# A hybrid layer stack with a selective scan on one core: ScalarE's share of stage work set by the kind of units, all front stages first, two turn stages beside others, a DRAM buffer for every image

## The chip, the cores and the metric

The kernel runs on one core of one Trainium2 chip. The core has a matrix engine (PE in the profile), VectorE (DVE), ScalarE (ACT), GpSimd (POOL), and SyncE (SP), which in this kernel issues every DMA. The metric is the device time of one execution in microseconds; the number that counts is the median of several runs.

## The reference

Four images of 96 channels and 64 x 64 pixels pass through four layers. Cut to what is computed:

```python
# layer 0: group norm, 1x1 conv to 192 channels, depthwise 3x3, silu, then a selective scan
u  = silu(depthwise3x3(Win @ gn(x)) + conv_b)            # (b, 192, 64, 64)
xs = [u by rows, u by columns, both of them reversed]    # K = 4 sequences of L = 4096
dt, B, C = split(sel_w[k] @ xs[k])                       # 6, 16 and 16 rows
delta = softplus(dt_w[k] @ dt + dt_b)
h[t]  = h[t-1] * exp(delta[t] * A) + (delta[t] * xs[t]) * B[t]   # 192 channels x 16 states
y[t]  = sum over the states of h[t] * C[t]  (+ Ds * xs)
x = x + Wout @ layernorm(y0 + y1 + y2 + y3, turned back to rows)
# layer 1: inverted residual: 1x1 conv to 576, depthwise 3x3, 1x1 conv back, residual
# layer 2: spectral block: w1, relu, FFT over 4096 tokens, complex diagonal, relu, inverse FFT, w2;
#          then a feed-forward with values rounded to 8-bit floats
# layer 3: attention without softmax (6 heads), then a second such feed-forward
```

The scan of layer 0 has 4 images x 4 sequences x 192 channels x 16 states, each 4096 steps long. It is most of the work.

## The kernel before

**Units of the scan.** `scans` cuts the scan into steps of 512 positions: 4 images x 4 sequences x 8 chunks = 128 steps. Every step has 12 units of two 128 x 512 tiles (a tile is 32 channels x 4 states), so there are 1536 units; the text calls the turn of the main loop that starts unit n "slot n". One unit costs: a product `db` on GpSimd (L1266); two `exp` on ScalarE (L1276, function `decays`) into PSUM tiles `ps_da`; two scans on VectorE (L1285, function `states`); a product with C, which gives `hc`; and eight small matmuls that sum over the states for a pair of units (L1330). Two kinds of unit alternate. In a "pool" unit (numbers 1, 3, 5, 7 and 10 of 12, `POOL_C`) GpSimd makes the product with C (L1306) and copies the last state (L1302). In the other seven, VectorE makes the product (two L1290) and ScalarE copies the last state (two L1300, function `keep`). `ps_da` has four banks, which is two units.

**ScalarE's order.** Inside a slot the kernel emits, in this order: `decays` for the next unit, ahead of which stand the copies `keep` of the previous one if that was not a pool unit; the copy `yt` of finished sums (L1344, function `sums_out`); the inputs of later units; the scans of this unit; sums; and at last the stage work. Every engine runs its instructions in the order written.

**Stages.** All other work is cut into streams of small pieces, grouped into stages: `front` (input convolution, silu, and the scan's inputs delta, delta times u, B and C, which are stored to DRAM as `d_delta`, `d_du` and `d_bc`), `turn` (adds the column sequences' outputs, turned back to rows, to the others), `conv` (layer norm of layer 0's output and layer 1), two `spectral` stages, `layer_2`, `product` and `layer_3`. A stage begins when the stage before it has ended; inside a stage up to `width` streams run side by side. `middle(b)` is turn and conv of image b, `layers_2_and_3(b)` the rest; `plan` lists the stages. The turn of images 2 and 3 already runs beside layer 3 of the image before, as stage `layer_3_turn`; the turn of images 0 and 1 is a stage of its own with one stream.

**The planner.** Each piece names an engine and a rough cost in microseconds. At the end of each slot `advance` takes pieces from the first stage's streams for as long as the budget `owed` lasts (`RATE`, 6.0 per slot, more near the end) and the piece fits its engine's `room`. Room grows in each slot by the first number of `SHARE` and is capped by the second: for ScalarE 2.4 and 2.8. A piece fits if room is at least half of its cost. So `SHARE` says how much stage work stands between the `decays` of two slots. When the scan has ended, what is left of the last image (`behind`, and layers 2 and 3 of image 3) is emitted with nothing beside it.

**Buffers.** `big` gives two large SBUF tiles (6144 floats per partition); a front holds both, as `ua` and `ub`, and uses 4096 columns of each. `turn` takes one as `ya`. `tmp` is a ring of 10 tiles of 512 columns. `d_delta`, `d_du` and `d_bc` have three images' worth in DRAM, so image 3 takes image 0's place.

Of the kernel before, what the change touches and what calls it, by code (L numbers as in the profile page):

```python
# [27 lines left out]
B, C, H, W = 4, 96, 64, 64  # L28
L = H * W
# [22 lines left out]


WORK = {"weights": 47.0, "turn": 79.2, "front": 417.0, "conv": 447.0,
        "spectral": 111.2, "layer_2": 231.0, "product": 1.2, "layer_3": 153.6, "layer_3_turn": 232.8}
RATE = 6.0
SHARE = {"pe": (3.0, 3.2), "act": (2.4, 2.8), "dve": (1.5, 2.0)}
NQ, NG, NPAIR = 4, HID // 32, H // 2


# [35 lines left out]
def hybrid_kernel(ctx: ExitStack, tc: tile.TileContext, a: dict):  # L96
# [111 lines left out]
    def images(name, shape, zero=None, sets=2):  # L208

        out = []  # L210
        for i in range(sets):
            t = dram1.tile(shape, F32, name=f"{name}{i}")
            if zero is not None:
                zero(t)
            out.append(t)
        return out

    d_delta = [images(f"delta{k}_", [NCH, DI, CH], sets=3) for k in range(K)]
    d_du = [images(f"du{k}_", [NCH, DI, CH], sets=3) for k in range(K)]
    d_bc = [images(f"bc{k}_", [NCH, 2 * NS, CH], sets=3) for k in range(K)]  # L220

# [353 lines left out]

    def scan_inputs(b, u, o, c, done):

        i = b % 3  # L580
        if not done.issuperset([c] if o == 0 else range(NCH)):
            while not done.issuperset([c] if o == 0 else range(NCH)):
                yield wait(1)
            yield wait(2)
        ua, ub = u
        yield pe(1.8, 1)
        p = bank()
        mm(p, lhsT=sel[:, o, 0, :], rhs=view(ua, o, c), start=True, stop=False)
        mm(p, lhsT=sel[:, o, 1, :], rhs=view(ub, o, c), start=False, stop=True)

        yield ac(0.7)
        xd = tmp("xd")
        act(xd, p, AF.Identity, bias=col("one"))
        free()
        for e in (0, 1):
            later(d_bc[o + 2 * e][i][c], xd[64 * e : 64 * e + 2 * NS])
        for part in range(3):
            yield pe(0.9, 1, part > 0)
            p = bank()
            if part < 2:  # L600
                mm(p, lhsT=dtw[:, o + 2 * part, 0:128], rhs=xd, start=True, stop=True)  # L601
                at = [(slice(0, 128), o + 2 * part, slice(0, 128))]
            else:
                for e in (0, 1):
                    mm(p[64 * e : 64 * e + 64], lhsT=dtw[:, o + 2 * e, 128:DI], rhs=xd, start=True, stop=True)
                at = [(slice(64 * e, 64 * e + 64), o + 2 * e, slice(128, DI)) for e in (0, 1)]

            yield ac(0.65)
            z = tmp("z")
            act(z, p, AF.Abs)  # L610
            yield ac(0.65)
            act(z, z, AF.Exp, scale=-1.0)
            yield ac(0.65)
            act(z, z, AF.Ln, bias=1.0)  # L614
            yield dv(0.7)
            nc.vector.scalar_tensor_tensor(p, p, 0.0, z, ALU.max, ALU.add)  # L616
            yield dv(0.85)
            g = tmp("g")
            nc.vector.tensor_mul(split(g), split(p), view(ub if part == 2 else ua, o, c))
            for rows, k, ch in at:  # L620
                later(d_du[k][i][c][ch], g[rows])
            yield ac(0.6)
            nc.scalar.copy(z, p)  # L623
            free(behind=True)
            for rows, k, ch in at:
                later(d_delta[k][i][c][ch], z[rows])
        traced[b].add((o, c))

    def turn(b):


        im = b % 2
        early = b == B - 1
        while scanned[b] < (2 if early else 3) * NCH:
            yield wait(1)
        t = big("ya")
        for r in (2, 0, 1) if early else (0, 1, 2):
            lo = 64 * r
            for at, k in ((0, 1), (64, 3)):
                load(t[at : at + 64, :L].rearrange("p (c l) -> p c l", c=NCH),  # L640
                     d_y[k][im][:, lo : lo + 64, :].rearrange("c p l -> p c l"))

            rows = not (early and r == 2)
            held = slice(0 if rows else 64, 128)

            def fetch(c):
                u = t[:, L + c % 4 * CH : L + c % 4 * CH + CH]
                if rows:
                    load(u[:64], d_y[0][im][c, lo : lo + 64])
                load(u[64:], d_skip[b][c, lo : lo + 64])  # L650
                return u

            def added(p, of):
                c, u = of
                mm(split(p[:64]), lhsT=const("two")[:, :64],  # L655
                   rhs=t[:, :L].rearrange("p (w h) -> p h w", h=H)[:, c * RPC : (c + 1) * RPC, :], start=True, stop=False)
                mm(p[:64], lhsT=skips[held, r], rhs=u[held], start=False, stop=True)

            def stored(p, of):
                s = tmp("yrow")[:64]  # L660
                nc.scalar.copy(s, p[:64])
                later(d_yt[im][of[0]][lo : lo + 64], s)

            chunks = ahead(1, fetch, range(NCH))

            ready = (lambda n: scanned[b] >= 2 * NCH + min(n + 2, NCH)) if early and rows else (lambda n: True)
            yield wait(10)
            yield from in_turn(chunks, pe(2.7, 1), added, ac(0.6), stored, ready=ready)
            yield wait(2)

# [398 lines left out]
    def layers_2_and_3(b):  # L1069
# [83 lines left out]
        else:  # L1153
# [1 line left out]
        return spectra + [  # L1155
            Stage("layer_2", 4 if b == B - 1 else 3, *(layer_2(c) for c in range(NCH))),
            Stage("product", 1, product()),
            Stage("layer_3", 4 if b == B - 1 else 3, *(layer_3(c) for c in range(NCH))) if b not in (1, 2) else
            Stage("layer_3_turn", 4, turn(b + 1), *(layer_3(c) for c in range(NCH))),
        ]  # L1160

    def front(b):


        u, there, done = [], set(), set()

        def memory():
            u.extend([big("ua")[:, :L], big("ub")[:, :L]])
            if b > 0:
                yield from normalised(b, arriving(b), there)  # L1170
                return

            chunks = [(c, fetch_image(b, c, tmp)) for c in range(NCH)]
            load(cst[:, CS["grp"]], a["cst"][:, CS["grp"]])
            load(cols, a["cols"])
            first_weights()
            yield from group_norm(b, chunks)
            yield from normalised(b, chunks, there)

        streams = [memory()]  # L1180
        for c in range(0, NCH, 2):
            streams.append(input_conv(b, u, c, there, done))
            for e in (c, c + 1):
                streams.append(scan_inputs(b, u, 0, e, done))
        streams += [scan_inputs(b, u, 1, c, done) for c in range(NCH)]
        return [Stage("front", 3 if b == 0 else 4, *streams)]


# [5 lines left out]

    def middle(b):

        return ([] if b >= 2 else [Stage("turn", 1, turn(b))]) + conv_block(b)

    def plan():

        stats = (group_norm(b, arriving(b)) for b in range(1, B))
        out = [Stage("weights", 2, later_weights(), *stats)] + front(1) + front(2)
        out += middle(0) + layers_2_and_3(0) + front(3)
        for b in (1, 2):
            out += middle(b) + layers_2_and_3(b)
        return out

    def scans(stages):
# [22 lines left out]

        def load_states(step, j):
            t = pair("rep_BC")
            of = d_bc[step["k"]][step["b"] % 3][step["c"], 8 * j : 8 * j + 8].rearrange("(s e) l -> s (e l)", e=2)
            load(t.rearrange("p e l -> p (e l)"), of.unsqueeze(0).to_broadcast([32, 4, 2 * CH]))
            step["BC"][j] = t

        def load_channels(step, i, name):
            t = pair(f"rep_{name}")
            of = (d_delta if name == "d" else d_du)[step["k"]][step["b"] % 3][step["c"], 64 * i : 64 * i + 64]  # L1240
            load(t.rearrange("p e l -> p (e l)"),
                 of.rearrange("(p e) l -> p (e l)", e=2).unsqueeze(1).to_broadcast([32, 4, 2 * CH]))
            step[name][i] = t
# [95 lines left out]
        def sums_out():  # L1339
            while summed:  # L1340
                group, y = summed.pop(0)
                step = group[0]["step"]
                yt = sp.tile([128, CH], F32, name="yt")
                nc.scalar.copy(yt, y)  # L1344
                to = d_y[step["k"]][step["b"] % 2][step["c"]]
                for m in (0, 1):
                    at = 128 * group[0]["pass"] + 64 * m
# [13 lines left out]
        for slot in range(len(units) + 6):  # L1361
# [26 lines left out]
                states(x)  # L1388
            for group in due.get(slot, ()):
                sums(group)  # L1390
            for e, (us, most) in SHARE.items():
                room[e] = min(room[e] + us, most)
            tensor[0] = 0.0
            held_banks[0] -= freed[0]
# [8 lines left out]


    clock, tensor = [-1], [0.0]
    room = {e: most for e, (_, most) in SHARE.items()}

    class Stage:

# [233 lines left out]
```

## Time and profile before

| what | value |
|---|---|
| median of 3 runs | 6344.4 us (6340.63 to 6344.61) |
| the profiled execution | 6358.61 us, its span 6356.8 us |
| first scan to last scan's unit | 81.2 to 5912.6 us of the span |
| after the scan | 444.2 us |
| VectorE busy | 5490.6 us (86% of the span) |
| GpSimd busy | 5169.6 us (81%) |
| ScalarE busy | 4191.3 us (66%) |

All times below are of the span. VectorE's instructions L1285 come two per unit, so their order in the trace tells when each slot began; with the order of the program, this gives each stage's slots and times:

| stage | slots | from, to (us) | us per slot |
|---|---|---|---|
| front of images 1 and 2 | 112 to 305 | 617.3 to 1418.4 | 4.15 |
| turn of image 0 | 305 to 355 | 1418.4 to 1593.4 | 3.50 |
| conv of image 0 | 355 to 489 | 1593.4 to 2046.1 | 3.38 |
| spectral of image 0, two stages | 489 to 557 | 2046.1 to 2307.4 | 3.84 |
| layer_2 of image 0 | 557 to 619 | 2307.4 to 2531.3 | 3.61 |
| layer_3 of image 0 | 626 to 669 | 2554.1 to 2709.8 | 3.62 |
| front of image 3 | 669 to 769 | 2709.8 to 3116.6 | 4.07 |
| turn of image 1 | 769 to 819 | 3116.6 to 3300.6 | 3.68 |
| layer_3_turn (images 1 and 2) | 1089 to 1147 | 4274.9 to 4504.7 | 3.96 |
| conv of image 3, up to the last unit | 1477 to 1536 | 5709.6 to 5912.6 | 3.44 |

In the profile's groups, "out<-in xcount | busy, mean ns" is followed by the idle time of the engine just ahead of these instructions and by what ended it. In windows, each row is a stretch with the busy time and number of instructions of every engine, the granted clock of the matrix engine, the share of the DMA engines and GB/s.

### The profile page before, as it was taken

Reading aid. Unit: us, or ns where it says so; the run is one execution under the profiler, and the core shown is the slowest. Engines: PE = TensorE matmul, PEld = TensorE weight load, DVE = VectorE, ACT = ScalarE, POOL = GpSimd, SP = SyncE. Lnnn points to the kernel's source line nnn. Section 1 sums busy time; section 2 is a strip of 40 time slices with the busy share of each in tenths; the row PEclk is TensorE's granted clock in tenths of the full one; section 3 lists DMA queues with packets and bytes.
Section 4 is the critical chain, followed back from the end, with each engine's and each line's share of the span. In section 5 each row is a group of like instructions: output and inputs, shape, how many; then the busy total and the mean of one; then the engine's idle time right before and its main releaser. Section 6 shows DMA issues by size and latency. Waiting matters only on the chain. (4 is left out here: it accounts for less than half of the span.)

```text
span 6356.8 us, 84759 instructions
## 1 busy us (share of the span) xinstructions
PE 4685.7 (74%) x27692; PEld 1723.3 (27%) x27692; DVE 5490.6 (86%) x6059; ACT 4191.3 (66%) x8072; POOL 5169.6 (81%) x2743
## 2 busy tenths in 40 slices
PE   6732767756888776686469878767898777679998
PEld 2100212201222642121012236321222552112274
DVE  4979898998999989989989998888999999889245
ACT  5743777765666677877546656767666667666435
POOL 4857878779999899987899998898999988889100
PEclk9855978867998888797779987878899887789999
DMA  5654565667754554456776445456754554566201
GB/s 178 206 167 146 190 204 187 201 201 221 221 162 151 183 181 156 151 193 208 212 213 197 156 152 192 157 162 199 225 171 159 171 192 141 172 209 202 84 13 39
DMA packets 430397, 1100.47 MB, mean 173 GB/s; under 512 B 74138, under 2 KB 75904, under 8 KB 428804
## 3 DMA queue, kind: packets, MB, share of 16 engines
q1 hardware_dynamic: 429956, 1095.06, 54.3%
q8 instruction: 220, 3.60, 0.2%
q14 instruction: 221, 1.81, 0.1%
HBM read 861.88 MB, written 237.44 MB: 173 GB/s over the span
## 5 line engine op out<-in xcount | busy, mean ns | idle before, releaser
L1266 POOL TENSOR_TENSOR db<-rep_g,rep_BC 128x1024 f32<-128x1024 f32 x1536 | 3607.0, 2365 | 689.1 <-DVE hc L1285 323.5
L1276 ACT ACTIVATE ps_da<-rep_d,aneg 128x512 f32<-128x512 f32 x3072 | 2061.8, 690 | 478.8 <-DVE hc L1285 347.2
L1285 DVE TENSOR_TENSOR_SCAN ps_da<-ps_da,state,db 128x512 f32<-128x512 f32 x1568 | 1923.9, 1272 | 274.3 <-ACT state L1300 151.4
L1306 POOL TENSOR_TENSOR hc<-hc,rep_BC 128x1024 f32<-128x1024 f32 x640 | 1511.2, 2361 | 49.3 <-DVE hc L1285 4.5
L1285 DVE TENSOR_TENSOR_SCAN hc<-ps_da,state,db 128x512 f32<-128x512 f32 x1120 | 1371.7, 1266 | 71.3 <-issue 20.6
L1330 PE MATMUL ps_y<-hc,cst 128*32 128x512 f32 x6144 | 1014.4, 739 | 566.2 <-POOL hc L1306 261.1
L1290 DVE TENSOR_TENSOR hc<-ps_da,rep_BC 128x512 f32<-128x512 f32 x1792 | 1135.5, 675 | 0.0
L1300 ACT COPY state<-ps_da 128x1 f32<-128x1 f32 x1568 | 246.3, 157 | 456.9 <-DVE hc L1290 455.4
L1330 PEld LDWEIGHTS ps_y<-hc,cst 128*32 128x32 f32 x6144 | 145.8, 118 | 1210.5 <-issue 438.2
L810 PE MATMUL ps_mm<-h,wd 128*32 128x512 f32 x3120 | 357.0, 593 | 7.0 <-ACT r L155 7.0
L550 PE MATMUL ps_mm<-xp,taps 128*128 128x512 f32 x576 | 294.7, 656 | 54.9 <-ACT ua L552 15.1
L1285 DVE TENSOR_TENSOR_SCAN ps_da<-ps_da,db 128x512 f32<-128x512 f32 x224 | 261.3, 1212 | 39.5 <-ACT state L1300 24.7
L787 PE MATMUL ps_mm<-wd,w 128*32 128x512 f32 x1984 | 254.9, 630 | 29.3 <-DMA wd<-x 20.0
L601 PE MATMUL ps_mm<-xd,dtw 128*128 128x512 f32 x256 | 168.5, 751 | 73.6 <-ACT z L623 53.5
L791 ACT ACTIVATE h<-ps_mm 128x512 f32<-128x512 f32 x261 | 151.8, 597 | 66.5 <-PE ps_mm L787 64.5
L869 PE MATMUL ps_mm<-r,cst 128*128 128x512 f32 x222 | 152.3, 778 | 56.5 <-ACT acc L892 14.2
L616 DVE SCALAR_TENSOR_TENSOR ps_mm<-ps_mm,z 128x512 f32<-128x512 f32 x192 | 131.7, 686 | 70.8 <-ACT z L614 67.0
L1285 DVE TENSOR_TENSOR_SCAN hc<-ps_da,db 128x512 f32<-128x512 f32 x160 | 186.2, 1204 | 6.1 <-issue 3.1
L655 PE MATMUL ps_mm<-ya,cst 128*64 128x512 f32 x192 | 183.1, 1044 | 10.4 <-ACT acc L892 10.4
L610 ACT ACTIVATE z<-ps_mm 128x512 f32<-128x512 f32 x192 | 114.1, 595 | 111.7 <-PE ps_mm L601 59.2
L982 PE MATMUL ps_mm<-wa,xp 128*64 128x96 f32 x1728 | 134.9, 318 | 64.6 <-DVE d L987 61.9
L550 PEld LDWEIGHTS ps_mm<-xp,taps 128*128 128x128 f32 x576 | 115.9, 208 | 229.5 <-issue 159.9
(348 smaller groups left out, 6675.9 us busy)
## 6 DMA issues: line engine op xcount, KB each, us to landing
rep_BC<-bc SPq DMA_DIRECT2D x512, 512.0 KB
rep_g<-du SPq DMA_DIRECT2D x384, 512.0 KB
rep_d<-delta SPq DMA_DIRECT2D x384, 512.0 KB
y<-yt SPq DMA_DIRECT2D x512, 128.0 KB
du<-g SPq DMA_DIRECT2D x128, 256.0 KB
delta<-z SPq DMA_DIRECT2D x128, 256.0 KB
tab<-in_etab SPq DMA_DIRECT2D x112, 256.0 KB
ya<-y SPq DMA_DIRECT2D x24, 1024.0 KB
```

The costliest lines, as they stand in the source:

```text
L550: mm(p, lhsT=taps[:, t, 0:128], rhs=window(t, c + e), start=t == 0, stop=t == 8)
L601: mm(p, lhsT=dtw[:, o + 2 * part, 0:128], rhs=xd, start=True, stop=True)
L655: mm(split(p[:64]), lhsT=const("two")[:, :64], rhs=t[:, :L].rearrange("p (w h) -> p h w", h=H)[:, c * RPC : (c + 1) * RPC, :], start=True, ...
L787: mm(p[32 * n : 32 * n + 32], lhsT=w1[:, 32 * g : 32 * g + 32], rhs=xin[:, n : n + 15 : 2, 1 : W + 1], start=True, stop=True)
L810: mm(p[32 * n : 32 * n + 32], lhsT=held["wd"][:, groups[i], o, dx, :], rhs=here[i][:, :, dx : dx + W], start=dx == 0, stop=dx == 2)
L1266: nc.gpsimd.tensor_mul(x["db"], x["step"]["g"][x["i"]], both(x["step"]["BC"][x["j"]][:, 0]))
L1276: act(x["da"][e], x["step"]["d"][x["i"]][:, e], AF.Exp, scale=aneg[:, av : av + 1])
L1285: nc.vector.tensor_tensor_scan(x["h"][e][:, order], x["da"][e][:, order], x["db"][:, e, order], start, ALU.mult, ALU.add)
L1290: x["made"] = nc.vector.tensor_mul(x["hc"][:, e], x["h"][e], x["step"]["BC"][x["j"]][:, 1])
L1300: nc.scalar.copy(to[:, e : e + 1], x["h"][e][:, end : end + 1])
L1306: x["made"] = nc.gpsimd.tensor_mul(x["hc"], x["hc"], both(x["step"]["BC"][x["j"]][:, 1]))
L1330: done = mm(y[32 * q : 32 * q + 32], lhsT=const("stack"), rhs=x["hc"][:, e], start=first or (x["pass"] == 0 and x["j"] == 0), stop=last or ...
```

## The change

Five edits:

- **ScalarE's share** depends on two things: whether this slot's unit is a pool unit, and whether the next one is. Pool then not pool: 2.8 per slot, capped at 3.0. Not pool then pool: 1.2, capped at 1.6. Two alike: 2.4 and 2.8, as before.
- The copy of finished sums on ScalarE takes 0.6 from ScalarE's room.
- **All fronts first**: the front of image 3 follows that of image 2, ahead of the conv of image 0.
- **Two turns moved**: the turn of image 0 runs as a second stream of image 3's front, in the unused columns of `ua` and `ub` (two halves of 2048 columns each, so its loads and its strided matmuls come in two halves; its small input `u` comes from the `tmp` ring). The turn of image 1 runs beside layer 3 of image 0, as the others did.
- `d_delta`, `d_du` and `d_bc` have an image's worth of DRAM for each of the four images.

```diff
-SHARE = {"pe": (3.0, 3.2), "act": (2.4, 2.8), "dve": (1.5, 2.0)}
+SHARE = {"pe": (3.0, 3.2), "dve": (1.5, 2.0)}
+SHARE_ACT = {(True, False): (2.8, 3.0), (True, True): (2.4, 2.8), (False, False): (2.4, 2.8), (False, True): (1.2, 1.6)}
...
-    d_delta = [images(f"delta{k}_", [NCH, DI, CH], sets=3) for k in range(K)]
+    d_delta = [images(f"delta{k}_", [NCH, DI, CH], sets=B) for k in range(K)]
...
-        i = b % 3
+        i = b
...
-    def turn(b):
+    def turn(b, rooms=()):
...
-        t = big("ya")
+        if rooms:
+            of_rows = [t[:, L:] for t in rooms]
+        else:
+            t = big("ya")
+            of_rows = [t[:, :L]]
+        each = L // len(of_rows)
...
-            for at, k in ((0, 1), (64, 3)):
-                load(t[at : at + 64, :L].rearrange("p (c l) -> p c l", c=NCH),
-                     d_y[k][im][:, lo : lo + 64, :].rearrange("c p l -> p c l"))
+            for n, part_of in enumerate(of_rows):
+                cs = slice(n * each // CH, (n + 1) * each // CH)
+                for at, k in ((0, 1), (64, 3)):
+                    load(part_of[at : at + 64].rearrange("p (c l) -> p c l", l=CH),
+                         d_y[k][im][cs, lo : lo + 64, :].rearrange("c p l -> p c l"))
...
-                u = t[:, L + c % 4 * CH : L + c % 4 * CH + CH]
+                u = tmp("yu") if rooms else t[:, L + c % 4 * CH : L + c % 4 * CH + CH]
...
-                mm(split(p[:64]), lhsT=const("two")[:, :64],
-                   rhs=t[:, :L].rearrange("p (w h) -> p h w", h=H)[:, c * RPC : (c + 1) * RPC, :], start=True, stop=False)
-                mm(p[:64], lhsT=skips[held, r], rhs=u[held], start=False, stop=True)
+                wide_of = W // len(of_rows)
+                mm(p[:64], lhsT=skips[held, r], rhs=u[held], start=True, stop=False)
+                for n, part_of in enumerate(of_rows):
+                    mm(split(p[:64])[:, :, n * wide_of : (n + 1) * wide_of], lhsT=const("two")[:, :64],
+                       rhs=part_of.rearrange("p (w h) -> p h w", h=H)[:, c * RPC : (c + 1) * RPC, :], start=False,
+                       stop=n == len(of_rows) - 1)
...
-            Stage("layer_3", 4 if b == B - 1 else 3, *(layer_3(c) for c in range(NCH))) if b not in (1, 2) else
+            Stage("layer_3", 4 if b == B - 1 else 3, *(layer_3(c) for c in range(NCH))) if b == B - 1 else
             Stage("layer_3_turn", 4, turn(b + 1), *(layer_3(c) for c in range(NCH))),
...
+        if b == B - 1:
+            return [Stage("front_turn", 5, streams[0], turn(0, rooms), *streams[1:])]
         return [Stage("front", 3 if b == 0 else 4, *streams)]
...
-        return ([] if b >= 2 else [Stage("turn", 1, turn(b))]) + conv_block(b)
+        return conv_block(b)
...
-        out = [Stage("weights", 2, later_weights(), *stats)] + front(1) + front(2)
-        out += middle(0) + layers_2_and_3(0) + front(3)
+        out = [Stage("weights", 2, later_weights(), *stats)] + front(1) + front(2) + front(3)
+        out += middle(0) + layers_2_and_3(0)
...
                 nc.scalar.copy(yt, y)
+                room["act"] -= 0.6
...
-            for e, (us, most) in SHARE.items():
+            of = (x is not None and x["pool"], slot + 1 < len(units) and units[slot + 1]["pool"])
+            for e, (us, most) in (SHARE | {"act": SHARE_ACT[of]}).items():
                 room[e] = min(room[e] + us, most)
```

More of the change, by code (lines that the diff above doesn't have):

```diff
@@ L54 @@
 WORK = {"weights": 47.0, "turn": 79.2, "front": 417.0, "conv": 447.0,
-        "spectral": 111.2, "layer_2": 231.0, "product": 1.2, "layer_3": 153.6, "layer_3_turn": 232.8}
+        "spectral": 111.2, "layer_2": 231.0, "product": 1.2, "layer_3": 153.6, "layer_3_turn": 232.8, "front_turn": 496.2}
 RATE = 6.0
-SHARE = {"pe": (3.0, 3.2), "act": (2.4, 2.8), "dve": (1.5, 2.0)}
+SHARE = {"pe": (3.0, 3.2), "dve": (1.5, 2.0)}
+SHARE_ACT = {(True, False): (2.8, 3.0), (True, True): (2.4, 2.8), (False, False): (2.4, 2.8), (False, True): (1.2, 1.6)}
 NQ, NG, NPAIR = 4, HID // 32, H // 2
@@ L216, in images @@
         return out
-    d_delta = [images(f"delta{k}_", [NCH, DI, CH], sets=3) for k in range(K)]
-    d_du = [images(f"du{k}_", [NCH, DI, CH], sets=3) for k in range(K)]
-    d_bc = [images(f"bc{k}_", [NCH, 2 * NS, CH], sets=3) for k in range(K)]
+    d_delta = [images(f"delta{k}_", [NCH, DI, CH], sets=B) for k in range(K)]
+    d_du = [images(f"du{k}_", [NCH, DI, CH], sets=B) for k in range(K)]
+    d_bc = [images(f"bc{k}_", [NCH, 2 * NS, CH], sets=B) for k in range(K)]
     d_y = [images(f"y{k}_", [NCH, 256, CH]) for k in range(K)]
@@ L1162, in front @@
     def front(b):
-        u, there, done = [], set(), set()
+        u, rooms, there, done = [], [], set(), set()
         def memory():
-            u.extend([big("ua")[:, :L], big("ub")[:, :L]])
+            rooms.extend([big("ua"), big("ub")])
+            u.extend([t[:, :L] for t in rooms])
             if b > 0:
@@ L1233, in load_states @@
             t = pair("rep_BC")
-            of = d_bc[step["k"]][step["b"] % 3][step["c"], 8 * j : 8 * j + 8].rearrange("(s e) l -> s (e l)", e=2)
+            of = d_bc[step["k"]][step["b"]][step["c"], 8 * j : 8 * j + 8].rearrange("(s e) l -> s (e l)", e=2)
             load(t.rearrange("p e l -> p (e l)"), of.unsqueeze(0).to_broadcast([32, 4, 2 * CH]))
@@ L1239, in load_channels @@
             t = pair(f"rep_{name}")
-            of = (d_delta if name == "d" else d_du)[step["k"]][step["b"] % 3][step["c"], 64 * i : 64 * i + 64]
+            of = (d_delta if name == "d" else d_du)[step["k"]][step["b"]][step["c"], 64 * i : 64 * i + 64]
             load(t.rearrange("p e l -> p (e l)"),
@@ L1405, in hybrid_kernel @@
     clock, tensor = [-1], [0.0]
-    room = {e: most for e, (_, most) in SHARE.items()}
+    room = {e: most for e, (_, most) in SHARE.items()} | {"act": 2.8}
     class Stage:
```

## The prediction

> **What bounds the kernel now.** I read the busy shares first, then windows cut where the scan begins and ends, then VectorE's waits, then windows by stage.
>
> ```profile
> PE 4685.7 (74%) x27692; PEld 1723.3 (27%) x27692; DVE 5490.6 (86%) x6059; ACT 4191.3 (66%) x8072; POOL 5169.6 (81%) x2743
> ```
>
> Two engines are near the top, VectorE and GpSimd. Cutting the span at the first scan and after the last unit:
>
> ```profile
> 81.20:5912.60 5831.40, 4222.50 (x23410) 1470.96 (x23412) 5311.74 (x5729) 3981.36 (x7745) 5157.52 (x2735) 0.82 0.58 183
> 5912.60:6356.80 444.20, 412.64 (x4154) 231.67 (x4146) 164.20 (x301) 181.64 (x286) 0.00 (x0) 0.98 0.14 43
> ```
>
> The third busy time is VectorE's: 5311.7 of 5831.4 us while the scan runs, so 519.7 us idle. In the second row it is hardly used; there the matrix engine works 412.6 of 444.2 us. So the time of the scan part is VectorE's busy time plus its idle time, and PE sets the rest. VectorE's own waits say what the idle time is:
>
> ```profile
> DVE ps_da L1285 <- ACT state L1300: 176.1, 111, 10.5
> DVE ps_da L1285 <- ACT ps_da L1276: 56.8, 40, 4.4
> DVE st L501 <- DMA x<-in_x: 40.5, 1, 40.5
> DVE ps_da L1285 <- POOL db L1266: 38.8, 34, 7.6
> DVE ps_mm L616 <- ACT z L614: 30.3, 20, 4.0
> ```
>
> Over 230 us are scans that wait for ScalarE, though ScalarE is the less busy engine: it is late, not full. Three stages, in windows:
>
> ```profile
> 1418.40:1593.40 175.00, 102.86 (x296) 18.17 (x296) 154.11 (x160) 89.00 (x191) 167.90 (x93) 0.72 0.71 212
> 1593.40:2046.10 452.70, 392.91 (x2280) 114.35 (x2280) 430.76 (x466) 302.25 (x595) 449.03 (x237) 0.91 0.58 181
> ...
> 4274.90:4504.70 229.80, 172.06 (x455) 39.74 (x454) 192.98 (x202) 165.24 (x330) 195.51 (x105) 0.82 0.67 198
> ```
>
> First a turn alone: GpSimd is busy 168 of 175 us, VectorE 154. Then a conv, where GpSimd is full (449 of 453). Then layer 3 with a turn, where neither is (VectorE 193 of 230). In the turn ScalarE has little to do (89 us), and still scans wait for it. The reason is in ScalarE's waits there:
>
> ```profile
> ACT yrow L661 <- PE ps_mm L657: 42.9, 20, 14.0
> ACT state L1300 <- DVE hc L1290: 28.4, 14, 3.8
> ```
>
> ScalarE stands at the turn's eviction while PE waits for the turn's loads, and the next unit's `exp` stands behind it.
>
> **What the Trainium skill says.** "PSUM — Partial Sum Buffer", section "Engine vs sequencer instructions", has ScalarE's and VectorE's queues strictly first in, first out, and matmuls starting and ending in program order. The trace agrees: see L661 above. So stage work ahead of an `exp` delays a scan although ScalarE is 66% busy. "Perfetto Trace Analysis", section "Optimization Strategy", says that regimes with different contended engines can be improved by interleaving them. Here it bears on the turns: a slot asks 3.36 us of GpSimd (167.9/50 in the turn; 5157.5/1536 over all) and, without stage work, 3.08 of VectorE (154.1/50). In a turn or a conv GpSimd binds, in a front VectorE (379.9 of 416.9 us in 1001.5 to 1418.4). The 100 slots of the two turns so leave VectorE 100 x 0.28 = 28 us idle, which go if they run beside fronts and layer 3. That is part of the turns' idle time below and isn't added to it.
>
> **The change, part by part.** No scan work is added or taken away, so I sum three things: what moves behind the last scan, what VectorE's idle time becomes, and small additions.
>
> *1. What moves behind the scan.* ScalarE's income was 2.4 per slot. It becomes (5 x 2.8 + 5 x 1.2 + 2 x 2.4)/12 = 2.07, less two copies of 0.6 per 12 slots: 1.97. Stages that used it up get longer: in the two programs' order, fronts of images 1 and 2 take 105 and 107 slots instead of 91 each (112 to 203, 204 to 295), the six spectral stages 231 instead of 204 (waits between them included), layer_2 70 instead of 62. The two turns alone, 100 slots, go; image 3's front with a turn takes 119, each layer_3_turn 61 instead of 58. Summed, the conv of image 3 begins at slot 1499, before at 1477. It then moves at the same pace (3.3 planned us per slot in both), so more of it is left after the last unit. Counting matmuls after the last one of L1330: 2351 instead of 2178, 173 more. They are 84 of L810 (four run side by side), 64 of L787 (the same) and 25 of full width. Prices from the timeline of PE in this very stretch: 12 of L810 take 2.58 us (6015.24 to 6017.81), 4 of L787 take 0.87 us (6053.99 to 6054.87), one full one 0.86 us (6084.36 to 6085.22). Sum: 7 x 2.58 + 16 x 0.87 + 25 x 0.86 = 18.1 + 13.9 + 21.5 = 53.5 us. Nothing hides it: PE is busy 171.2 of 175.4 us in the stretch 5912.6 to 6088.0. +54 us. With it eight VectorE instructions of about 0.65 us leave the scan part: -5 us.
>
> *2. VectorE's idle time.* Stage work emitted in slot s stands ahead of the `exp` that the scan of slot s+2 needs. I took the idle time of VectorE ahead of each scan from the trace, and sorted it by kind of slot s, by stage, and by the planned ScalarE work of slot s. In all, 381 us (weights and product left out). Slots "not pool, then pool" carry 269 of it: 49 in fronts, 61 in spectral, 26 in layer_2, 33 in conv, 100 in turns and layer 3. There the `exp` of slot s+2 has only a pool unit's two scans (2 x 1.27 us) to hide in, and two state copies (0.16 each) precede it. In spectral the step is plain: 0 us per slot with up to 1.2 us planned, 0.68 with 1.8 to 2.4, 3.96 with 2.4 to 3.0. The new order puts at most 1.8 or so into such slots. Multiplying the new counts by the old means: fronts 29, spectral 1, layer_2 19, conv 31, layer 3 with turn 49, plus 10 that I take for the turn in the front: 139, so 130 less.
>
> The other slots carried 112 us (fronts 35, spectral 25, layer_2 13, conv 19, rest 20). Pool slots followed by another kind now get up to 3.0: some 87 slots at 3 us or more, of which the trace has few. Their price is open: 0.0 us in six spectral slots, 1.58 in six of front. So 0 to 137 us; I take 0.5 each, 44 us, since a long unit (two scans and two L1290, 3.9 us) then covers the `exp`. With the old means for the rest I get 138 us, 26 more.
>
> Together 104 us less. A cruder sorting without stages gives 64 for the shares alone. I take 85, with 15 to 150 as ends: turns that stall behind their loads do so beside layer 3 too (36.8 and 42.3 us of idle time in the two layer_3_turn stages, 8.2 in the layer_3 alone, about 18 and 20 in the turns), so there the sorting is the least sure.
>
> *3. Additions with one answer.* Image 0's turn in halves: 24 more matmuls (L655 takes 1035 ns for 512 strided columns, so halves cost about the same together; PE has slack there) and six more loads (626 ns of SP each, spread over 119 slots): 0; uncovered, 6 x 0.63 = 4 us. Fourth DRAM images: other addresses, no instruction; without them image 3's front, at slot 338, would overwrite what the scan of image 0 still reads, up to slot 384. The turn's input in the `tmp` ring: its load waits on SP for a tile of ten uses back, with `rep` loads queued behind it, and GpSimd waits for those (the trace has 116.8 us of such waits on `rep_BC`, hidden mostly). Bound: 0 to 24 x 1 us; I take 0.
>
> Sum on the profiled execution: 6356.8 + 54 - 5 - 85 = 6321 us of span, -36. The profiled run (6358.6) stands 14 us above the median 6344.4; applying -36 there gives **6308 us**.
>
> **Rivals.**
> *A, slower: the later conv decides.* The place is the stretch after the last scan, the price 54 us of PE work with nothing beside it. It decides as soon as idle time falls by less than 49 us. For it: stalls that come from PE and DMA stay, and the cap of 3.0 opens new ones; at 1.58 us per such slot part 2 gives only about 10 us. Against: the spectral numbers above. With 25 us regained: 6344 + 54 - 5 - 25 = 6368.
> *B, nothing: gain and cost cancel.* VectorE's work is the same, and a stall removed on ScalarE often becomes one on GpSimd (scans wait on `db` 57 us in all), and the four convs stay with GpSimd. 6344 +- 13.
> *C, much faster.* If alternating shares clear nearly all of the 230 us on ScalarE, idle time falls by 150 or more: 6344 + 49 - 150 = 6243. Against: turns' waits on loads, 40.5 us of the weights stage (loads of rows on SP), which nothing touches.
> That the turns aren't really interleaved is excluded by the order of instructions.
>
> **How the numbers follow.** Forecast 0.48, A 0.26, B 0.14, C 0.12. Range: my ends for idle time, 15 to 150, give 6378 and 6243; cutting the rare tail of C, 6255 to 6378. A measurement of this kernel tells 0.2% (13 us) from no change; faster is the forecast and C, 0.60, same 0.14, slower 0.26.
>
> **What would show it.** Scans' waits on `state` L1300 and on `ps_da` should fall from 233 us to about 150; spectral windows from 3.84 us per slot to about 3.6; the stretch after the last unit should grow from 444 to about 498 us, nearly all PE; layer_3_turn should come three times with 25 to 40 us idle each. The prediction is wrong if the stretch after the scan grows by much less than 54 us, if scans still wait on ScalarE for 200 us, or if GpSimd's waits on `rep` grow in the front with a turn.

## The result, and the profile after

The changed kernel takes 6329.83 us (median of 13 runs, 6317.88 to 6334.25). The kernel before, run beside it 13 times, takes 6335.24 us (6323.9 to 6344.61). The ratio is 0.999, with a 95% interval of 0.9981 to 0.9998: some 5 us, where 36 us were forecast. The profiled execution of the changed kernel took 6329.87 us (span 6328.1), which is its median. That of the kernel before, 6358.6 us, was 23 us above its own median.

The changed kernel in windows, cut at the first scan and at the end of the last one (columns as before: stretch, its length, then busy time of PE, PE's weight loads, VectorE, ScalarE and GpSimd, the granted clock, DMA share, GB/s):

```profile
79.30:5828.10 5748.80, 4136.25 (x23110) 1441.46 (x23106) 5300.57 (x5720) 3958.34 (x7709) 5159.94 (x2735) 0.83 0.58 186
5828.10:6328.10 500.00, 469.38 (x4505) 250.84 (x4504) 170.20 (x311) 203.80 (x321) 0.00 (x0) 0.99 0.13 41
```

Beside the two rows of before: the scan part went from 5831.4 to 5748.8 us, and VectorE's idle time in it (length less busy time) from 519.7 to 448.2 us. The stretch behind the last scan went from 444.2 to 500.0 us, and PE is busy in all but 31 us of it. So both things happened that the prediction summed. VectorE's waits while the scan runs show where the idle time changed:

```profile
DVE ps_da L1299 <- ACT ps_da L1290: 70.1, 39, 9.7
DVE ps_da L1299 <- ACT state L1314: 68.0, 45, 8.2
DVE hc L1299 <- issue: 60.3, 44, 13.2
DVE hc L1299 <- ACT ps_da L1290: 54.2, 18, 6.9
DVE st L502 <- DMA x<-in_x: 41.0, 1, 41.0
```

L1299 is the scan (L1285 before), L1314 the state copy, L1290 the `exp`. The wait on state copies fell from 176.1 to 68.0 us. But scans that write `hc`, which are those of the pool units, now wait 54.2 us for the `exp`, and 60.3 us for something that the view doesn't name ("issue"). The same two waits in the kernel before:

```profile
DVE hc L1285 <- issue: 23.7, 32, 3.0
DVE hc L1285 <- ACT ps_da L1276: 9.2, 4, 3.0
```

The timeline settles the unnamed one: each of these 44 scans of the changed kernel starts 0.09 us after an `exp` has ended, so they waited for ScalarE too. The late work moved from the one kind of unit to the other.

By stage, VectorE's idle time, the first trace of before against the changed kernel: fronts of images 1 and 2, 65 to 39 us; spectral 87 to 64; layer_2 56 to 27. Against that, the front of image 3 and the turn of image 0, 51 us as two stages, became 69 as one; and layer_3, the turn of image 1 and two layer_3_turn, 119 us, became three layer_3_turn with 126.

### The profile page after: what moved, and what is told of

It is laid out like the page before. It is cut to its first block, busy times and chain, and to the rows that moved or that the text cites. A ratio compares the mean times of both kernels' runs of the same rounds, so it can differ in the third digit from the quotient of the medians.

```text
span 6328.1 us, 84866 instructions
## 1 busy us (share of the span) xinstructions
PE 4655.2 (74%) x27740; PEld 1712.8 (27%) x27740; DVE 5485.5 (87%) x6059; ACT 4190.5 (66%) x8072; POOL 5171.6 (82%) x2743
## 5 line engine op out<-in xcount | busy, mean ns | idle before, releaser
L1290 ACT ACTIVATE ps_da<-rep_d,aneg 128x512 f32<-128x512 f32 x3072 | 2063.6, 689 | 507.8 <-DVE hc L1299 361.0
L1299 DVE TENSOR_TENSOR_SCAN ps_da<-ps_da,state,db 128x512 f32<-128x512 f32 x1568 | 1921.2, 1270 | 143.5 <-ACT ps_da L1290 54.0
L1299 DVE TENSOR_TENSOR_SCAN hc<-ps_da,state,db 128x512 f32<-128x512 f32 x1120 | 1371.0, 1265 | 135.6 <-issue 57.2
L1314 ACT COPY state<-ps_da 128x1 f32<-128x1 f32 x1568 | 245.5, 157 | 410.5 <-DVE hc L1304 408.4
L821 PE MATMUL ps_mm<-h,wd 128*32 128x512 f32 x2976 | 342.0, 592 | 7.0 <-ACT r L156 7.0
L551 PE MATMUL ps_mm<-xp,taps 128*128 128x512 f32 x576 | 287.9, 641 | 44.6 <-ACT xp L531 26.3
L1299 DVE TENSOR_TENSOR_SCAN ps_da<-ps_da,db 128x512 f32<-128x512 f32 x224 | 261.1, 1210 | 52.8 <-ACT state L1314 17.6
L798 PE MATMUL ps_mm<-wd,w 128*32 128x512 f32 x1848 | 231.1, 607 | 15.2 <-ACT h L802 11.8
L1299 DVE TENSOR_TENSOR_SCAN hc<-ps_da,db 128x512 f32<-128x512 f32 x160 | 186.2, 1204 | 26.2 <-ACT ps_da L1290 16.0
L1036 PE MATMUL ps_mm<-z,tab 128*128 128x96 f32 x864 | 133.9, 322 | 55.9 <-DMA tab<-in_etab 41.5
```

The source lines that it names most:

```text
L551: mm(p, lhsT=taps[:, t, 0:128], rhs=window(t, c + e), start=t == 0, stop=t == 8)
L798: mm(p[32 * n : 32 * n + 32], lhsT=w1[:, 32 * g : 32 * g + 32], rhs=xin[:, n : n + 15 : 2, 1 : W + 1], start=True, stop=True)
L821: mm(p[32 * n : 32 * n + 32], lhsT=held["wd"][:, groups[i], o, dx, :], rhs=here[i][:, :, dx : dx + W], start=dx == 0, stop=dx == 2)
L1290: act(x["da"][e], x["step"]["d"][x["i"]][:, e], AF.Exp, scale=aneg[:, av : av + 1])
L1299: nc.vector.tensor_tensor_scan(x["h"][e][:, order], x["da"][e][:, order], x["db"][:, e, order], start, ALU.mult, ALU.add)
L1314: nc.scalar.copy(to[:, e : e + 1], x["h"][e][:, end : end + 1])
```

## Experiments

The table has all of them. "Scan part", "idle" (of VectorE in it) and "behind" (after the last scan) are windows of one profiled execution of each; ratios are to the kernel before, run beside them on the same chip.

| kernel | median us | ratio (95% interval) | scan part | idle | behind |
|---|---|---|---|---|---|
| before, first trace | 6335.24 | 1 | 5831.4 | 520 | 444 |
| before again (e1) | 6333.19 | 1.0001 (0.9992 to 1.0010) | 5799.1 | 489 | 446 |
| changed | 6329.83 | 0.9990 (0.9981 to 0.9998) | 5748.8 | 448 | 500 |
| shares alone (e2) | 6490.82 | 1.0245 (1.0232 to 1.0259) | 5664.4 | 367 | 751 |
| order alone (e3) | 6384.63 | 1.0072 (1.0057 to 1.0087) | 5860.9 | 551 | 440 |
| changed, loads split (e4) | 6277.10 | 0.9907 (0.9893 to 0.9920) | 5684.0 | 378 | 505 |
| e4, small loads ahead (e5) | 6231.82 | 0.9837 (0.9821 to 0.9854) | 5653.4 | 341 | 505 |
| e5, old shares (e6) | 6275.00 | 0.9909 (0.9894 to 0.9923) | 5757.5 | 454 | 436 |
| e5, shares between (e7) | 6217.40 | 0.9815 (0.9798 to 0.9831) | 5703.0 | 400 | 439 |
| e5, more in long units (e8) | 6238.07 | 0.9847 (0.9831 to 0.9863) | 5703.1 | 394 | 447 |
| before, loads split and ahead (e9) | 6268.64 | 0.9897 (0.9881 to 0.9914) | 5740.9 | 439 | 443 |

VectorE's busy time in the scan part lies between 5297.6 and 5312.1 us in all of them. So, to within 15 us, the scan part's length is read from the idle column alone.

### e1: the kernel before, once more

No edit.

> The kernel before, unchanged, to see how far two executions of one program differ. Theory T (the gain was priced on a trace of an execution that was itself 20 us longer than is typical): time equals before within 0.2%, but the span of this profile, about 6325 to 6345 us, is shorter than the 6356.8 us of the first, and the difference lies in VectorE's idle time while the scan runs, below 519.7 us. Rival R (the first profile was typical, and the change lost its 30 us somewhere that its trace doesn't show): the span is again 6350 to 6360 us with about 520 us idle.

```profile
80.80:5879.90 5799.10, 4171.66 (x23397) 1449.31 (x23396) 5310.17 (x5728) 3980.42 (x7743) 5158.96 (x2735) 0.83 0.57 184
5879.90:6325.60 445.70, 413.88 (x4165) 232.37 (x4163) 165.54 (x304) 182.68 (x288) 0.00 (x0) 0.99 0.13 42
```

These are the windows of its second trace. The span is 6325.6 us instead of 6356.8, the stretch behind the scan is the same, and VectorE's idle time is 488.9 us instead of 519.7. Theory T holds: one program's idle time differs by 31 us between two executions. The difference has no single place: of it, 14 us are in the spectral stages and 10 in layer_2. What makes it differ stays open. One thing goes with it: PE was busy for 4222.5 us of the scan part in the first execution and for 4171.7 in the second, at a mean granted clock of 0.834 and 0.843. In the 14 executions of e1, the two with the highest mean clock (0.843) took 6323 and 6327 us, the five with 0.836 or 0.837 took 6331 to 6346. Whether a lower clock makes the stalls or only comes with them isn't shown.

### e2: the shares alone

```diff
-SHARE = {"pe": (3.0, 3.2), "act": (2.4, 2.8), "dve": (1.5, 2.0)}
+SHARE = {"pe": (3.0, 3.2), "dve": (1.5, 2.0)}
+SHARE_ACT = {(True, False): (2.8, 3.0), (True, True): (2.4, 2.8), (False, False): (2.4, 2.8), (False, True): (1.2, 1.6)}
...
                 nc.scalar.copy(yt, y)
+                room["act"] -= 0.6
```

> The kernel before with ScalarE's new shares and the charge of 0.6 alone; order of stages and turns as before. In the order of the program 498 more matmuls stand behind the last scan than in before, which at the prices of the prediction are 274 us of PE. Theory T (shares remove idle time in fronts, spectral and layer_2, some 80 us, and pay for it with a later last stage): 6335 + 274 + layer 3 of image 2, also behind the scan, about 50 - 130 = 6500 to 6560 us. VectorE's idle time per slot: fronts about 0.18 (before 0.33), spectral about 0.3 (before 0.43), layer_2 about 0.15 (before 0.30). Rival R (the idle time fell because stages were spread and reordered, not by the shares): idle time per slot in these stages stays as before, and the time is 6600 us or more.

6490.82 us, 9 us under T's range and far from R's. Idle time per slot: fronts of images 1 to 3, 0.16 us (52 us in 330 slots); spectral 0.21; layer_2 0.17. So the shares themselves take idle time away, with the stages where they were. But the stages no longer fit: 751 us lie behind the last scan instead of 446, and nearly all of the last layer_3_turn is among them, so the idle time of 367 us isn't that of the same work. In the old order these shares lose more than they win; milder ones, as in e7, weren't tried in it.

### e3: the order alone

```diff
-SHARE = {"pe": (3.0, 3.2), "dve": (1.5, 2.0)}
-SHARE_ACT = {(True, False): (2.8, 3.0), (True, True): (2.4, 2.8), (False, False): (2.4, 2.8), (False, True): (1.2, 1.6)}
+SHARE = {"pe": (3.0, 3.2), "act": (2.4, 2.8), "dve": (1.5, 2.0)}
...
                 nc.scalar.copy(yt, y)
-                room["act"] -= 0.6
```

(against the changed kernel)

> The changed kernel with the old ScalarE shares and without the charge: all fronts first, two turns beside other stages, four DRAM images. 40 matmuls fewer than before stand behind the last scan (-9 us). Theory T (a turn beside a stage stalls as long or longer than alone, since its loads delay the other stage's): idle time 60 to 80 us in the front with a turn and about 40 us in each of three layer_3_turn stages, against 155 us in before for front of image 3, both turns, layer_3 and two layer_3_turn; so 6335 - 9 + 40 = about 6365 us, 6345 to 6385. Rival R (interleaving itself wins the 28 us that VectorE lost in the turns alone): 6335 - 9 - 28 = about 6298 us.

```profile
79.90:5940.80 5860.90, 4209.65 (x23525) 1465.80 (x23522) 5309.75 (x5728) 3984.73 (x7745) 5159.66 (x2735) 0.82 0.57 182
5940.80:6380.30 439.50, 408.39 (x4090) 233.09 (x4088) 165.64 (x304) 181.15 (x285) 0.16 (x1) 0.98 0.14 43
```

0.7% slower, at the upper edge of T. VectorE is idle for 551 us. The front with a turn has 81 us of that, the three layer_3_turn 41, 41 and 52. The 28 us that VectorE lost beside GpSimd in the turns alone don't show as a gain. The test is not a clean one, though. With the old shares the plan comes to the second layer_3_turn at slot 1007, and the turn of image 2 must wait for its column sequences, which the scan reaches only at slot 1056. By the order of the program, layer 3 is nearly all emitted before that turn begins, and its last 65 slots of 114, with the turn as good as alone, hold 35 of the 41 us. The same happens in e6. The change splits into two halves that nearly cancel: the order costs about 50 us, and on top of it the shares win about 55 (6384.6 to 6329.8), being 103 us less idle time for 60 us more behind the scan.

### e4: the turn's loads cut into eight

First the place in the changed kernel where a layer_3_turn begins. SP's queue, in order of time (start, duration, line, what is loaded, how many):

```profile
2973.40 1.29 SPq L648 DMA_DIRECT2D ya<-y  x2
2974.79 3.58 SPq L955 DMA_DIRECT2D xc<-x  x3
```

Two loads of 1 MB for the turn, and behind them layer 3's small inputs. PE, ScalarE, GpSimd and VectorE there (the brackets have the idle time ahead of an instruction and what ended it):

```profile
2996.23 2.02 PE L948 MATMUL ps_mm<-xc,cst 96*96 96x512 f32 x2 [14.17 <-DMA xc<-x]
```

```profile
2998.29 0.68 ACT L950 ACTIVATE xc<-ps_mm,cols 96x512 f32<-96x512 f32 x1 [11.76 <-PE ps_mm L948]
2998.87 1.29 ACT L1290 ACTIVATE ps_da<-rep_d,aneg 128x512 f32<-128x512 f32 x2
```

```profile
2998.61 2.35 POOL L1280 TENSOR_TENSOR db<-rep_g,rep_BC 128x1024 f32<-128x1024 f32 x1 [8.70 <-DMA rep_BC<-bc]
```

```profile
2999.65 2.47 DVE L1299 TENSOR_TENSOR_SCAN ps_da<-ps_da,state,db 128x512 f32<-128x512 f32 x2 [8.36 <-ACT ps_da L1290]
```

Read upward: the scan stood 8.36 us for its `exp`; the `exp` stood in ScalarE's queue behind an eviction of layer 3; that waited 11.76 us for a PE product; and PE had waited 14.17 us for `xc`, whose load was issued behind the turn's 2 MB. How much ScalarE work the plan puts into the slot isn't what decides here: ScalarE itself was idle for those 11.76 us. GpSimd's line shows a second path from the same place: it waited 8.70 us for the scan's own input `rep_BC`. A stall of 7 to 10 us comes at the same three places of all three layer_3_turn stages.

```diff
-            for n, part_of in enumerate(of_rows):
-                cs = slice(n * each // CH, (n + 1) * each // CH)
-                for at, k in ((0, 1), (64, 3)):
-                    load(part_of[at : at + 64].rearrange("p (c l) -> p c l", l=CH),
-                         d_y[k][im][cs, lo : lo + 64, :].rearrange("c p l -> p c l"))
+            for c in range(NCH):
+                part_of = of_rows[c * CH // each][:, c * CH % each : c * CH % each + CH]
+                for at, k in ((0, 1), (64, 3)):
+                    load(part_of[at : at + 64], d_y[k][im][c, lo : lo + 64, :])
+                yield wait(1)
...
-            yield wait(10)
+            yield wait(2)
```

> The changed kernel, with each of a turn's loads of 1 MB cut into eight by chunk, one pair per slot, then a wait of two slots instead of ten; the rest of the order differs by no more than a few slots, and the last conv begins at the same slot 1499. Theory T (the stalls of about 8 us at the same three places of each layer_3_turn, and the one of 13 us at the start of the front with a turn, come from other loads that stand behind 2 MB of the turn's): these stalls fall below 3 us each, 50 to 80 us are won, 6250 to 6280 us. Rival R (they come from the turn's matmuls, 1035 ns each, or from its small loads one chunk ahead): the time stays within 15 us of the changed kernel's 6330.

6277.10 us, 53 us under the changed kernel, inside T's range. The first of the three stalls is gone in every layer_3_turn, and so is the one of 13.2 us at the start of the front with a turn. PE's wait for `xc` in the first layer_3_turn fell from 14.2 to 1.0 us at its longest. But two stalls of 6 to 8 us stay in each layer_3_turn. PE's waits in the first of these stages name them:

```profile
PE ps_mm L664 <- DMA ya<-skip: 20.9, 4, 9.2
```

### e5: the small loads further ahead

```diff
-            chunks = ahead(1, fetch, range(NCH))
+            known = not (early and rows)
+            chunks = ahead(2 if known else 1, fetch, range(NCH))
+            if known:
+                chunks = chain([next(chunks)], chunks)
```

(against e4; `known` leaves out the chunks of the last image that the scan may not have finished)

> The kernel of the split loads (6277 us), and in it the turn's small loads are issued two chunks ahead instead of one, the first of them before the wait of two slots; where the scan's chunk isn't known to be finished (last image, rows) it stays at one. Theory T (the stalls of 7 us that are left at two places of each layer_3_turn, and several of 3 to 6 us in the front with a turn, come from PE standing at the turn's first matmul until its small load has landed): these go, 35 to 60 us are won: 6217 to 6242 us. Rival R (they come from the turn's strided matmuls or from ScalarE): 6265 to 6285 us.

6231.82 us, inside T's range. In the first layer_3_turn no wait of VectorE is long now:

```profile
DVE hc L1302 <- issue: 4.8, 3, 2.9
DVE xq L889 <- ACT r L157: 3.0, 2, 2.8
DVE ps_da L1302 <- ACT ps_da L1293: 1.6, 3, 0.8
```

The three stages have 13, 8 and 21 us of idle time instead of 42, 41 and 43, and the front with a turn 46 instead of 69. One long stall is left, of 7.4 us in the third stage. It stands where the small loads stayed at one chunk ahead (last image, rows), which speaks for T once more. The scan part:

```profile
79.70:5733.10 5653.40, 4131.22 (x23106) 1431.35 (x23102) 5312.05 (x5720) 3957.31 (x7709) 5156.39 (x2735) 0.84 0.58 189
```

The idle time is 448 - 341 = 107 us less than in the changed kernel, and the four stages with a turn have just these 107 us less (194 to 87). So they came from the turns' loads.

### e6 to e8: the shares, with the loads mended

Against e5: e6 has the old shares (2.4 and 2.8 for every kind) and no charge. e7 and e8 differ by these lines:

```diff
# e7
-(False, True): (1.2, 1.6)}
+(False, True): (1.6, 1.8)}
...
-                room["act"] -= 0.6
# e8
-(True, False): (2.8, 3.0)
+(True, False): (3.2, 3.4)
```

> The kernel with loads split and ahead, but with the old ScalarE shares and no charge. Its order leaves 213 matmuls fewer behind the last scan than with the new shares (62 us of PE at the prices of the prediction). Theory T (the shares save about 110 us of idle time whatever the turns do, as between the order alone and the changed kernel): 40 to 60 us slower than the run with the loads ahead and the new shares. Rival R (a good part of that saving was that the turns' late loads hit less often; with the loads mended the shares save less than the 62 us that they cost behind the scan): equal to it or faster.

> Loads split and ahead, and shares between the two: 1.6 capped at 1.8 in slots not pool then pool, 2.8 capped at 3.0 in pool then not pool, and no charge for the copy of sums. The last conv begins at slot 1469, so behind the last scan stands as little as with the old shares (62 us less than with the new ones). Theory T (only what exceeds some 2 us of stage work in a slot before a pool unit stalls a scan): idle time grows by less than 30 us, and it is 30 to 55 us faster than the run with the loads ahead and the new shares. Rival R (every step above 1.2 per such slot costs): idle time grows by 60 us or more, no gain.

> Loads split and ahead, new shares, but 3.2 capped at 3.4 in slots pool then not pool. The last conv begins at slot 1474, with 54 us less behind the last scan than in the run with the loads ahead. Theory T (a long unit of 3.9 us covers the later exp): idle time grows by less than 25 us and it is 30 to 55 us faster than that run. Rival R (at 3 us and more each such slot costs 1.58 us, as in six slots of the first front of the kernel before): idle time grows by more than 54 us and nothing is won.

e6 is 43 us slower than e5: 113 us more idle time for 69 less behind the scan. T holds; the shares do their work whether or not turns stall. By stage, 40 of the 113 us lie in layer_2, 28 in the fronts of images 1 and 2, 27 in the three layer_3_turn (part of them where image 2's turn again runs after layer 3) and 18 in the convs, of which more lies inside e6's scan part; in the six spectral stages, where the prediction saw its plainest case, it is 2.

e7 is 14 us faster than e5. Neither theory fits: 66 us less behind the scan cost 59 us of idle time, nearly R's 60, but there is a small gain. It is the fastest of all, 1.85% under the kernel before. Its windows:

```profile
77.60:5780.60 5703.00, 4177.63 (x23525) 1463.51 (x23522) 5302.64 (x5728) 3983.38 (x7745) 5157.92 (x2735) 0.83 0.58 187
5780.60:6219.90 439.30, 408.19 (x4090) 232.61 (x4088) 165.64 (x303) 181.04 (x285) 0.13 (x1) 0.98 0.14 43
```

e8 lies 6 us above e5, within what runs differ: 58 us less behind the scan, 53 us more idle time. T was wrong there; the long unit doesn't cover the later `exp` for free. R was right that nothing would be won, and its 54 us of idle time were nearly reached; the price per slot that it named wasn't measured. More stage work per slot and less behind the scan trade nearly one for one here.

### e9: the kernel before, with the loads mended

The edits of e4 and e5, on the turn of the kernel before.

> The kernel before, with its own order and shares, and only the turn's loads split and ahead. The last conv begins at slot 1477 as in before. Theory T (a turn's loads stall scans wherever the turn stands): idle time in the two layer_3_turn stages falls from 77 us to about 30 and in the two turns alone from 48 to about 30, 55 to 75 us are won: 6260 to 6280 us, which is the same as with all fronts first, old shares and the same loads (6275 us), so that the order by itself wins nothing. Rival R (only turns beside other stages collide with loads, so that the order plus mended loads is the gain): 6290 us or more.

6268.64 us, 1.0% under before, and within 7 us of e6, which has the changed order and the same shares and loads. Idle time is 33 us in the two layer_3_turn (77 in e1) and 24 in the two turns alone (48). So the loads stalled scans wherever a turn stood, in the kernel before too, and the order by itself wins nothing even with the loads mended, as far as e6 tells, which gives up the place of image 2's turn beside layer 3. What the order does is make room for the shares: e2 has them without it and pays behind the scan, e5 has both.

## Why the prediction was wrong

The measured 6329.83 us lie inside the range that the prediction gave, but the gain of 36 us that it forecast isn't there: 5 us were measured.

*Behind the last scan: +54 us.* Right, in mechanism and size. The conv of image 3 begins at slot 1499, and the stretch from the end of the last scan grew by 54.3 us (445.7 in e1, 500.0 in the changed kernel), nearly all PE.

*VectorE's busy time: -5.* It fell by 10 to 11 us against the two traces of before. Small.

*VectorE's idle time: -85.* This is the step that failed, in the place where it says "Multiplying the new counts by the old means". Against the second trace of before the idle time fell by 41 us, not 85. Of the 44 us that are missing, 31 are the base that the sum stood on. The other 13 are what is left of larger errors that nearly cancelled:

- The base. The means were taken from an execution with 520 us of idle time; the second has 489. That execution was 23 us above the median of 13 runs, and the prediction put it at 14 above the three runs shown and carried its gain over undiminished. But stalls that a particular execution had on top, those in spectral and layer_2, are just the ones that the sorting let vanish. Against the very trace that it was priced on, the span fell by 29 us where 36 were forecast. That nearness is luck, as the next points show.
- The other kinds of slot. "With the old means for the rest I get 138 us, 26 more": sorted in the same way, they went from 113 to 233 us, 120 more. The slots "not pool, then pool" did nearly what was forecast. They went from 275 us in the first trace (the prediction's sorting gave 269) and 256 in the second to 124, with 139 forecast. So late work was moved, where the prediction took it for removed. Spectral shows it best: the first kind fell there from 59 to 13 us, but the others rose from 24 to 47.
- The turns. Of those 120 us, 83 lie in the four stages that have a turn; for the same work the other kinds went from 29 to 112 us. The first kind has 68 us there, near its price (49 and 10, and a part of the fronts' 29). The sorting took stalls in turns for a matter of how much ScalarE work stands in a slot. e4 and e5 show that they come from the turn's loads: 2 MB ahead of another stage's inputs, and small loads one chunk ahead. With these mended, the 112 us are 58 and the 68 are 19. Moved turns took their stalls along. The prediction had read this chain in the profile (ScalarE's wait for L657) and still priced it by ScalarE's share. (Its "about 18 and 20 in the turns" are also read too low: in the windows of its own stage table they are 20.9 and 31.2 us.)
- What the sum put at nothing. Idle time ahead of VectorE's stage work (softplus, layer norms) fell by 30 to 40 us. Without this the miss would have been larger.

Sorted by what it waits for, VectorE's idle time in the scan part is this (us; an unnamed wait is counted to ScalarE where an `exp` ended less than 0.15 us ahead of the scan):

| VectorE idle | before | e1 | changed | e3 | e6 | e5 |
|---|---|---|---|---|---|---|
| scans, for ScalarE | 279 | 273 | 282 | 312 | 249 | 178 |
| scans, for others | 109 | 96 | 74 | 91 | 80 | 72 |
| ahead of stage work | 131 | 121 | 92 | 148 | 125 | 91 |

The prediction named two waits that should fall from 233 us to about 150, and they did, to 138. But with the pool units' waits counted, scans stood for ScalarE as long as before. So its own sign of being wrong, "if scans still wait on ScalarE for 200 us", came true. Only with the loads mended does this row fall clearly, and then the shares show in it (e6 to e5). The layer_3_turn stages came three times as said, with 42, 41 and 43 us each, just above the 25 to 40 that it named.

*Rivals.* What happened is closest to B, gain and cost cancel, but by another way than B named: GpSimd's part didn't grow (scans' wait on `db` fell, 38.8 to 26.3 us in the larger row, and all their waits on GpSimd from 100 us in the first trace and 85 in the second to 60); ScalarE's stalls came back at the pool units and with the turns. Rival A's price and place were right. By its point of decision, 49 us of regained idle time, it should have come, since only 41 came back; VectorE's busy time gave 10 us where 5 were counted, and so the two nearly balance.

Not tried: the rest of the idle time in the front with a turn (46 us in e5, 15 and 21 in the plain fronts), for which the `tmp` ring, the halved loads and the streams' number are all candidates. e4 cuts the loads and spreads them over slots at once; which of the two helps, and whether the small loads are late because of their place in the queue or because the DMA engines are full (91% busy from 2970 to 3000 us, with this one queue), wasn't taken apart. The change also put the small input's matmul ahead of the strided one in every turn, so that PE meets the small load earlier; its share in the stalls isn't known.

## What to carry to other kernels

Where one engine's idle time is to be priced from a trace, trace the same program twice first: a sum of stalls has to allow for an error of at least that difference, 31 us here. A stall that reads "waits for ScalarE" must be followed to its first cause; here VectorE, ScalarE and PE stood in a row behind two large loads, and cutting these gave ten times what the whole change gave. When a wait is made shorter at one kind of instruction, look at the same wait at all the others before calling it gone. And pacing work more gently beside a bound engine isn't free if what is left over runs alone at the end: 60 us behind the scan paid for 103 us in it.

## What the runs showed of the hardware

Three inputs of layer 3, issued right behind two loads of 1 MB on the same queue, kept PE waiting 14.17 us; with the 2 MB issued as sixteen loads over eight slots, PE's wait on `xc` is 1.0 us there. The same program, executed twice, differed by 31 us of VectorE's idle time at a mean granted PE clock of 0.834 and 0.843; which of the two comes first, these traces don't show.
